# Weights turned during the forward pass, a PSUM bank for each half of the mixing, small loads on ScalarE's queue and an earlier table load, in a Hartley and AFNO expert kernel

## The chip, the cores and the metric

The kernel runs on one core of a Trainium2 chip. The metric is the device time of one execution in microseconds (us). A core has five engines that run side by side, each with its own instruction queue: TensorE (PE, matrix products into PSUM), VectorE (DVE), ScalarE (ACT), GpSimd (POOL) and SyncE (SP, here used to issue transfers). Any of ScalarE, GpSimd and SyncE can issue a transfer (DMA) between the chip's memory and SBUF; 16 DMA engines move the data.

## The reference

The input x is 16 images of 64 channels, 128 x 128 pixels, in float32 (67 MB). The reference first applies a spectral convolution and then an AFNO block with a mixture of experts:

```python
# spectral convolution: Hartley transform, 20 x 20 modes kept, weights w1 (64 x 64 x 20 x 20)
dht_2d(x) = fftn(x, axes=(2, 3)).real - fftn(flip(x, axis=(2, 3)), axes=(2, 3)).imag
x1n, x2n = _neg_k(x1), _neg_k(x2)
e = lambda a, b: einsum('bixy,ioxy->boxy', a, b)
mixed = 0.5 * (e(x1, x2) - e(x1n, x2n) + e(x1, x2n) + e(x1n, x2))
# (blurred along all four axes)
...
# the block
h = _group_norm(x, gn1_w, gn1_b)
h = _afno(h, afno_w1, afno_b1, afno_w2, afno_b2)
h = h + residual
...
feats = _gelu(_c1(h, fe_w, fe_b))
# shared and gated experts on feats
```

`_neg_k` maps the mode k to -k, so the mixing needs the weights twice: as they are, and turned.

## The kernel before

The kernel is one program with four stages that follow each other.

**Stage 1, the forward transform** (L194 to L263). The input comes in 128 tiles `xt` of 128 x 1024 (512 KB; a ring of 10 buffers, loaded by SP at L245). For each tile TensorE forms 16 small products with `fwd1` (L250) into one of four PSUM buffers, and ScalarE copies the result into `t1` (L253). Once the eight tiles of an image are done, a generator `along_columns` does the transform along the columns, interleaved with the tiles of the next image: TensorE L210 (with the table `fwd2`, loaded at L258 once the first image's tiles have been issued), ScalarE L215, VectorE L219 to L223, and then the blur over the images, which VectorE adds into `x2` (L231, L233). When an image of `x2` is complete, ScalarE writes its second half (L236, L237). At the end of the loop SP loads eleven rows of mixing weights into the lower 64 partitions of `wk` (L261).

**Stage 2, the mixing** (L265 to L341). Eleven rows of weights for the mode -k come into `wn` (L271, four buffers) and are copied in reversed order into the upper partitions of `wk` (L273, L274), by POOL for even rows and by ScalarE for odd rows. Then SP issues the transfer of `dev` (a table of the group norm) and 34 small loads (L276 to L301): `blurc`, `mean`, `gn1`, `ident`, `sel`, `vec` and 28 pieces of the AFNO weights. For each of the eleven rows k1 TensorE forms 20 products (L314) of 64 columns into one PSUM tile `psm`: the lower half of the partitions for even modes, the upper half for odd modes, both in one bank. ScalarE copies the lower half out (L318, L321, L322) and VectorE the upper half (L319, L323) to `om`. The channel blur (L332) turns `om` into `ot`, with copies on both engines (L339, L341). After it the table `spec` (3.2 MB, 100 partitions) and the expert weights `exw` are loaded (L344, L345).

**Stage 3, group norm statistics and AFNO** (L348 to L621). TensorE forms means (L420), deviations with `dev` (L430; ScalarE squares them, L432) and their sum (L436). A chain on VectorE gives the scales `gx` (L457 to L487). Then a loop over the 16 images: products of `ot` and `spec` (L599) in two halves of 512 columns, VectorE's scaled copy `xk` (L603) and ScalarE's plain copy `xr` (L604), both read from PSUM, then two AFNO layers (L537 to L552) and steps that prepare the inverse transform.

**Stage 4** (from L624) is the inverse transform, the features, the gate and the experts, in an order written out by hand: rows (L678), pixels (L704), features (L764), experts (L858 on TensorE, L863 on ScalarE, L866 on VectorE) and the stores (L877).

Each engine runs its instructions in the order of the program; a buffer that is used again waits for its last reader. Memory of a pool that is closed can be given to a later pool, whose first writer then waits for the last reader of the old one.

Of the kernel before, what the change touches and what calls it, by code (L numbers as in the profile page):

```python
# [11 lines left out]
F32 = mybir.dt.float32  # L12
AF = mybir.ActivationFunctionType
ALU = mybir.AluOpType
AX = mybir.AxisListType
PSUM = bass.MemoryType.PSUM
DRAM = bass.MemoryType.DRAM

NB, C, N = 16, 64, 128
K = 20  # L20
NM = K * K
CH = 100
MD = 32
W1 = 64
NE, TOPK = 16, 4
# [5 lines left out]
CL = C // 2  # L31
# [5 lines left out]
V_B1, V_SHB, V_EXB = 15, 17, 19  # L37
V_N = V_EXB + NE
# [120 lines left out]
def hartley_afno_moe_kernel(ctx: ExitStack, tc: tile.TileContext, a: dict, out: bass.AP):  # L159
    nc = tc.nc  # L160
# [11 lines left out]
        return t  # L172

    on_modes = ExitStack()
    otp = on_modes.enter_context(tc.tile_pool(name="ot", bufs=1, side="right"))
    ot = otp.tile([CH, 4, NB * C], F32, name="ot")

    od = dram.tile([NB, K, C, K], F32, name="od")
    ond = dram.tile([NB, K, C, K], F32, name="ond")
# [4 lines left out]
    exd = dram.tile([NE, C, C + 1], F32, name="exd")  # L184


    with tc.tile_pool(name="modes", bufs=1) as mp:


# [2 lines left out]
        wk = mp.tile([P, K // 2 + 1, K, C], F32, name="wk")  # L192
        gb = blur_matrix(NB)
        with tc.tile_pool(name="f_x", bufs=10) as xp, tc.tile_pool(name="f_t", bufs=2) as tp, \  # L194
                tc.tile_pool(name="f_c", bufs=1) as fc, \
                tc.tile_pool(name="f_p1", bufs=4, space=PSUM) as pp1, \
                tc.tile_pool(name="f_p2", bufs=2, space=PSUM) as pp2:
            fwd1 = load(fc, "fwd1", [P, W1], nc.gpsimd)
# [62 lines left out]
                nc.sync.dma_start(wk[0:C, k], a["w"][k])  # L261
            for _ in behind:
                pass  # L263

        with tc.tile_pool(name="m_o", bufs=1) as op, tc.tile_pool(name="m_w", bufs=4) as wp, \  # L265
                tc.tile_pool(name="m_p", bufs=2, space=PSUM) as pp, \
                tc.tile_pool(name="m_p2", bufs=4, space=PSUM) as pp2:

            for k in range(K // 2 + 1):
                wn = wp.tile([P, K, C], F32, name="wn")  # L270
                nc.sync.dma_start(wn[C:P], a["w"][(-k) % K])  # L271
                copy = nc.scalar.copy if k % 2 else nc.gpsimd.tensor_copy
                copy(wk[C:P, k, 0], wn[C:P, 0])  # L273
                copy(wk[C:P, k, 1:K], wn[C:P, K - 1:0:-1])  # L274
            sc = on_modes.enter_context(tc.tile_pool(name="s_c", bufs=1, side="right"))
            blurc = load(sc, "blurc", [P, C])  # L276
            dev = load(sc, "dev", [CH, 4, NM])
            mean = load(sc, "mean", [CH, 4, C])
            gn1 = load(sc, "gn1", [P, 2, C])
            ident = load(sc, "ident", [P, C])  # L280
            sel = load(sc, "sel", [CH, 5, 32])
            vec = load(const, "vec", [P, V_N])
            wx1 = sc.tile([P, 2, CL], F32, name="wx1")
            wx2 = sc.tile([P, 2, 2, CL], F32, name="wx2")
            bx1 = sc.tile([P, 2], F32, name="bx1")
            bx2 = sc.tile([P, 1], F32, name="bx2")
            v2s = a["v2"].rearrange("p (r h c) -> p h r c", r=2, h=2)
            for h in range(2):
                hs_ = slice(h * CL, (h + 1) * CL)
                for ri in range(2):  # L290
                    own_rows = slice(h * C + ri * CL, h * C + (ri + 1) * CL)
                    for ro in range(2):
                        c0 = (ri ^ ro) * P + h * CL
                        nc.sync.dma_start(wx1[own_rows, ro], a["w1"][hs_, c0:c0 + CL])
                    nc.sync.dma_start(bx2[own_rows], a["b2"][0:1, ri * C + h * CL:ri * C + (h + 1) * CL]
                                      .rearrange("a c -> c a"))
                    for j in range(2):
                        rows_j = slice(j * C + ri * CL, j * C + (ri + 1) * CL)
                        nc.sync.dma_start(wx2[rows_j, h],
                                          v2s[ri * C + h * CL:ri * C + (h + 1) * CL, h])  # L300
                        nc.sync.dma_start(bx1[rows_j, h:h + 1], a["vec"][hs_, V_B1 + ri:V_B1 + ri + 1])  # L301

            om = [op.tile([P, NB, NM // 2], F32, name=f"om{h}") for h in range(2)]
            lok, upk = (t[h * C:(h + 1) * C].rearrange("o b (k2 k1) -> o k1 k2 b", k1=K)
                        for h, t in enumerate(om))
            for k1 in range(K // 2 + 1):

                ps = pp.tile([P, K // 2, 2, NB, 2], F32, name="psm")  # L310
                for m in range(K // 2):
                    k = k1 * K + 2 * m
                    for h in range(2):
                        nc.tensor.matmul(ps[h * C:(h + 1) * C, m].rearrange("p a b q -> p (a b q)"),  # L314
                                         lhsT=wk[:, k1, 2 * m + h, :], rhs=x2[:, :, :, k:k + 2],
                                         start=True, stop=True)
                lo, up = ps[0:C, :, :, :, 0], ps[C:P, :, :, :, 1]
                nc.scalar.copy(lok[:, k1], lo[:, :, 0])  # L318
                nc.vector.tensor_copy(upk[:, k1], up[:, :, 0])  # L319
                if k1 % (K // 2):  # L320
                    nc.scalar.copy(lok[:, K - k1, 0:1], lo[:, 0:1, 1])  # L321
                    nc.scalar.copy(lok[:, K - k1, K // 2 - 1:0:-1], lo[:, 1:, 1])  # L322
                    nc.vector.tensor_copy(upk[:, K - k1, ::-1], up[:, :, 1])  # L323


            for b0 in range(0, NB, 8):
                for cc in range(2):
# [7 lines left out]
                    for h in range(2):  # L335
# [3 lines left out]
                            nc.scalar.copy(dst, src)  # L339
                        else:  # L340
                            nc.vector.tensor_copy(dst, src)  # L341

    sc2 = on_modes.enter_context(tc.tile_pool(name="s_c2", bufs=1, side="right"))
    spec = load(sc2, "spec", [CH, 4, 2 * MD * MD])  # L344
    exw = load(sc2, "exw", [P, C, NE])  # L345


    s3 = ctx.enter_context(ExitStack())  # L348
    pool = lambda name, bufs, **kw: s3.enter_context(tc.tile_pool(name=name, bufs=bufs, **kw))
# [44 lines left out]
    with tc.tile_pool(name="s_o", bufs=1) as so, \  # L394
# [3 lines left out]
        ones = sc.tile([P, C], F32, name="ones")  # L398
        nc.vector.memset(ones, 1.0)

        ext = sc.tile([C, NE, C + 1], F32, name="ext")
        nc.gpsimd.tensor_copy(ext[:, :, 0:C], exw[0:C].rearrange("p o e -> p e o"))
        nc.gpsimd.tensor_copy(ext[:, :, C], vec[0:C, V_EXB:V_EXB + NE])
        nc.gpsimd.dma_start(exd.rearrange("e i o -> i e o"), ext)
# [179 lines left out]
            return bn1s, bn1f, bn2s, bn2f  # L584

        sw = sq_pool.enter_context(tc.tile_pool(name="s_w", bufs=2))
        junk = sc.tile([P, MD * MD], F32, name="junk")
        first = second = None
        for b in range(NB):
            xk = sw.tile([P, MD * MD], F32, name="xk")  # L590
            xr = sw.tile([P, MD * MD], F32, name="xr")
            for n in range(2):
                cols = slice(n * 512, (n + 1) * 512)
                ps = pp2.tile([P, 512], F32, name="psx")
                for kc in range(4):
                    for h in range(2):
                        for ri in range(2):
                            p0 = h * C + ri * CL
                            nc.tensor.matmul(  # L599
                                ps[p0:p0 + CL], lhsT=ot[:, kc, b * C + h * CL:b * C + (h + 1) * CL],  # L600
                                rhs=spec[:, kc, ri * 1024 + n * 512:ri * 1024 + (n + 1) * 512],
                                start=(kc == 0), stop=(kc == 3))
                nc.vector.tensor_scalar(xk[:, cols], ps, gx[:, 0, b:b + 1], None, ALU.mult)  # L603
                nc.scalar.copy(xr[:, cols], ps)  # L604
                if n == 0:
                    nc.vector.tensor_scalar(xk[:, 0:1], xk[:, 0:1], gx[:, 1, b:b + 1], None, ALU.add)
                    if first:
                        second = layer1(*first)
                elif second:
                    layer2(*second)  # L610
            first = (b, xk, xr)
            if b == HB:
                bn1s, bn1f, bn2s, bn2f = prepare()
            if b < K // 2:
                modes(b)
            elif b < K // 2 + QB:
                modes_out(b - K // 2)
# [377 lines left out]
```

## Time and profile before

| | |
|---|---|
| three runs, median | 1709.37 us (1701.23 to 1716.32) |
| profiled execution, its own time | 1706.11 us |
| its span in the profile | 1704.3 us |
| mean granted TensorE clock | 0.972 |
| TensorE busy | 1564.1 us (92%) |
| ScalarE busy | 1314.3 us (77%) |
| VectorE busy | 1234.9 us (72%) |
| GpSimd busy | 153.3 us (9%) |
| first copy of stage 1 (L253) starts | 8.00 us |
| mixing's products (L314) run on from | 249.00 us |
| spectrum's products (L599) start | 311.80 us |
| stage 4 (L678) starts | 473.93 us |

The page also cuts the span in 40 equal slices of 42.6 us and gives the busy share of each in tenths (9 is 90% or more). The first six or seven slices are stages 1 and 2, the next four stage 3:

```profile
PE   6878758899978999999999999999999999999986
DVE  0344423455433888898988889898888889889998
ACT  2233334356656999999999999999999999999986
DMA  9899964333532425162442616244151533513123
```

The page's groups of instructions are read as: line, engine, operation, what it writes <- what it reads, shape, count | busy time in us, mean duration in ns | the idle time just before them, and what ended most of it. "issue" is time in which an engine waited for nothing that the profile shows. A line such as "SPq L245 <- PE ps L250" says that the transfer queue of SP, at line 245, waited for TensorE's instruction of line 250.

### The profile page before, as it was taken

How to read it: one execution, taken by the hardware profiler on the slowest of the kernel's cores; microseconds unless marked ns; L12 is line 12 of the kernel's file. 1: busy time of each engine (PE TensorE's matmuls, PEld its weight loads, DVE VectorE, ACT ScalarE, POOL GpSimd, SP SyncE). 2: the span in 40 equal slices, each digit the busy share in tenths (PEclk: the TensorE clock that was granted, in tenths of full speed). 3: DMA queues.
4: the chain of work that ended last, by engine and by line, in shares of the span. 5: the costliest groups of instructions: out<-in, count | busy, mean ns of one | idle time of the engine just before them, and what ended most of it. 6: DMA issues, size and time to landing. Idle time of an engine off the chain costs nothing.

```text
span 1704.3 us, 69104 instructions
## 1 busy us (share of the span) xinstructions
PE 1564.1 (92%) x31336; PEld 841.1 (49%) x31336; DVE 1234.9 (72%) x1584; ACT 1314.3 (77%) x1679; POOL 153.3 (9%) x137
## 2 busy tenths in 40 slices
PE   6878758899978999999999999999999999999986
PEld 6877755222276454545445454544545444454321
DVE  0344423455433888898988889898888889889998
ACT  2233334356656999999999999999999999999986
POOL 0000002002100110101011010101101011010110
PEclk9999979999988999999999999999999999999988
DMA  9899964333532425162442616244151533513123
GB/s 386 306 313 313 304 140 105 87 97 105 150 75 38 76 67 112 31 136 48 94 84 60 111 30 136 51 90 92 53 111 52 114 70 74 112 31 100 40 69 99
DMA packets 268973, 194.36 MB, mean 114 GB/s; under 512 B 228128, under 2 KB 229232, under 8 KB 268452
## 3 DMA queue, kind: packets, MB, share of 16 engines
q1 hardware_dynamic: 264984, 184.23, 42.7%
q0 software_dynamic: 3696, 5.71, 1.3%
q8 instruction: 246, 4.03, 1.0%
q14 instruction: 47, 0.39, 0.1%
HBM read 106.66 MB, written 83.23 MB: 111 GB/s over the span
## 4 chain that ended last, share of the span: by engine, by line
PE 84%; issue 7%; DVE 4%; ACT 2%; DMA 1%; POOL 0%; SPq 0%; DVEq 0%; POOLq 0%; ACTq 0%
PE pe L858 36%; PE pe L704 11%; PE pe L678 9%; PE psx L599 7%; PE pe L764 7%; PE ps L250 6%; PE ps L210 3%; DVE h L866 2%; PE psx L430 1%; PE pso L537 1%; PE pso L549 1%; DMA fwd_sb<-in_fwd_dram 1%; PE psd L517 1%; ACT g L863 1%; PE psm L314 0%
## 5 line engine op out<-in xcount | busy, mean ns | idle before, releaser
L866 DVE SCALAR_TENSOR_TENSOR h<-g,wt,h 128x1024 f32<-128x1024 f32 x512 | 625.3, 1279 | 53.7 <-ACT g L863 52.9
L863 ACT ACTIVATE g<-pe,wl 128x1024 f32<-128x1024 f32 x512 | 543.6, 1156 | 14.7 <-PE pe L858 14.0
L858 PE MATMUL pe<-f,wl 64*64 64x512 f32 x4096 | 498.3, 601 | 5.2 <-DMA wl<-exd,ati 3.2
L866 DVE SCALAR_TENSOR_TENSOR h<-g,h 128x1024 f32<-128x1024 f32 x256 | 300.9, 1216 | 37.6 <-ACT g L863 26.1
L863 ACT ACTIVATE g<-pe,vec_sb 128x1024 f32<-128x1024 f32 x256 | 274.0, 1116 | 26.6 <-PE pe L858 24.8
L858 PE MATMUL pe<-f,shw 64*64 64x512 f32 x2048 | 253.0, 602 | 0.0
L858 PEld LDWEIGHTS pe<-f,wl 64*64 64x64 f32 x4096 | 134.0, 132 | 231.5 <-ACT g L863 141.1
L704 PEld LDWEIGHTS pe<-inv_sb,u 64*64 64x64 f32 (+1 forms) x8192 | 195.8, 135 | 80.4 <-ACT g L863 52.3
L704 PE MATMUL pe<-inv_sb,u 64*64 64x128 f32 (+1 forms) x8192 | 203.7, 248 | 1.2 <-ACT u L685 1.2
L250 PE MATMUL ps<-fwd_sb,xt 128*64 128x64 f32 x4096 | 156.0, 233 | 34.7 <-issue 27.9
L678 PEld LDWEIGHTS pe<-inv_sb,bmf 64*64 64x64 f32 x4096 | 131.9, 137 | 85.2 <-issue 31.3
L678 PE MATMUL pe<-inv_sb,bmf 64*64 64x64 f32 x4096 | 152.6, 226 | 18.3 <-issue 16.4
L250 PEld LDWEIGHTS ps<-fwd_sb,xt 128*64 128x64 f32 x4096 | 145.5, 148 | 38.5 <-issue 31.5
L253 ACT COPY t<-ps 128x320 f32<-128x320 f32 x128 | 53.9, 426 | 141.7 <-PE ps L250 141.5
L685 ACT COPY u<-pe 128x1024 f32<-128x1024 f32 x128 | 130.8, 1042 | 36.3 <-PE pe L678 35.3
L678 PE MATMUL pe<-inv_sb,bmh 52*64 52x64 f32 x4096 | 146.6, 223 | 7.8 <-issue 7.8
L768 ACT ACTIVATE f<-pe,fba 128x1024 f32<-128x1024 f32 x128 | 145.7, 1170 | 3.0 <-PE pe L764 2.3
L710 DVE COPY h<-pe 128x1024 f32<-128x1024 f32 x64 | 78.4, 1225 | 74.3 <-PE pe L704 69.4
L764 PE MATMUL pe<-h,fsa 64*64 64x512 f32 x1024 | 131.7, 602 | 0.0
L678 PEld LDWEIGHTS pe<-inv_sb,bmh 52*64 52x64 f32 x4096 | 125.7, 137 | 10.4 <-issue 10.2
L831 POOL TENSOR_TENSOR dv<-root_e,dv 128x4 f32<-128x4 f32 x16 | 31.8, 1989 | 1038.1 <-DVE dv L830 1038.1
L599 PE MATMUL psx<-spec_sb,ot 100*32 100x512 f32 x1024 | 117.7, 602 | 7.4 <-issue 7.4
(181 smaller groups left out, 1112.5 us busy)
## 6 DMA issues: line engine op xcount, KB each, us to landing
xt<-in_x_dram SPq DMA_DIRECT2D x128, 512.0 KB
out_dram<-h SPq DMA_DIRECT2D x256, 256.0 KB
td<-tt SPq DMA_DIRECT2D x16, 512.0 KB
bmf<-td SPq DMA_DIRECT2D x16, 512.0 KB
bmh<-od SPq DMA_DIRECT2D x96, 50.0 KB
tnd<-tn SPq DMA_DIRECT2D x32, 128.0 KB
bmf<-td SPq DMA_DIRECT2D x32, 128.0 KB
bmf<-tnd SPq DMA_DIRECT2D x32, 128.0 KB
```

Source lines behind the costliest of these rows:

```text
L250: nc.tensor.matmul(ps[cols, i, :], lhsT=xt[:, i, cols], rhs=fwd1, start=True, stop=True)
L253: nc.scalar.copy(t1[:, :, c0:c0 + 8], src)
L599: nc.tensor.matmul(ps[p0:p0 + CL], lhsT=ot[:, kc, b * C + h * CL:b * C + (h + 1) * CL], rhs=spec[:, kc, ri * 1024 + n * 512:ri * 1024 + (n ...
L678: nc.tensor.matmul(ps[s * C:(s + 1) * C, h, i, part, :], lhsT=bmh[rs, c] if part else bmf[rs, c].rearrange("p r m -> p (r m)"), rhs=inv1[r ...
L685: nc.scalar.copy(dst, ps.rearrange("p h i q n -> p n q h i"))
L704: nc.tensor.matmul(to, lhsT=u[rs, (t * 4 + j) * 2 + half, part], rhs=by, start=(part == 0), stop=(part == 1))
L710: (nc.vector.tensor_copy if t % 2 else nc.scalar.copy)(h, ps)
L764: nc.tensor.matmul(ps[p * C:(p + 1) * C, half], lhsT=fsa[rows_, box["b"]], rhs=box["h"][t][rows_, p], start=True, stop=True)
L768: nc.scalar.activation(f, ps, AF.Gelu, bias=fba[:, box["b"]:box["b"] + 1], accum_out=box["sums"][:, t:t + 1])
L858: nc.tensor.matmul(ps[half * C:(half + 1) * C, p], lhsT=w[rows_], rhs=f[rows_, half], start=True, stop=True)
L863: nc.scalar.activation(g, ps, AF.Gelu, bias=bias)
L866: nc.vector.scalar_tensor_tensor(h, g, share(), h, ALU.mult, ALU.add)
```

## The change

The change has six parts.

1. A new pool `s_k` is opened ahead of everything, and the 34 small loads are issued by ScalarE at the very start of the program, instead of by SP in stage 2. Space for `ot` is taken only after the forward pass.
2. The loads of `wn` and the turning copies stand in the forward pass, after its last loads, with three buffers of a pool opened beside the x tiles (before: four buffers, in stage 2).
3. The mixing uses two PSUM tiles, `psm0` and `psm1`, one for each half; each product has 32 columns (its own modes only) instead of 64.
4. `dev`, `spec` and `exw` are loaded at the head of stage 2. `dev` and `spec` get memory that the pools of the forward pass held: in the built program `spec` waits for the last readers of the forward pass, and `dev` for the last turning copy; `dev` stands behind `spec` in SP's order.
5. `ext` and `junk`, two work tiles of stage 3, lie in other pools.
6. In the loop over images ScalarE's copy `xr` comes first, and VectorE's `xk` is made from `xr` in SBUF instead of from PSUM.

On ScalarE the program has 34 more instructions, on SP 34 fewer; on the other engines the numbers are unchanged. From L678 on the order on every engine is as before. The diff, cut:

```diff
     on_modes = ExitStack()
-    otp = on_modes.enter_context(tc.tile_pool(name="ot", bufs=1, side="right"))
-    ot = otp.tile([CH, 4, NB * C], F32, name="ot")
+    sk = on_modes.enter_context(tc.tile_pool(name="s_k", bufs=1, side="right"))
...
+    blurc = load(sk, "blurc", [P, C], nc.scalar)
+    mean = load(sk, "mean", [CH, 4, C], nc.scalar)
+    gn1 = load(sk, "gn1", [P, 2, C], nc.scalar)
+    ident = load(sk, "ident", [P, C], nc.scalar)
+    sel = load(sk, "sel", [CH, 5, 32], nc.scalar)
+    vec = load(const, "vec", [P, V_N], nc.scalar)
...
+                nc.scalar.dma_start(wx1[own_rows, ro], a["w1"][hs_, c0:c0 + CL])
...
-                tc.tile_pool(name="f_c", bufs=1) as fc, \
+                tc.tile_pool(name="f_c", bufs=1) as fc, tc.tile_pool(name="f_w", bufs=3) as wp, \
...
             for _ in behind:
                 pass
-
-        with tc.tile_pool(name="m_o", bufs=1) as op, tc.tile_pool(name="m_w", bufs=4) as wp, \
-                tc.tile_pool(name="m_p", bufs=2, space=PSUM) as pp, \
-                tc.tile_pool(name="m_p2", bufs=4, space=PSUM) as pp2:
-
             for k in range(K // 2 + 1):
                 wn = wp.tile([P, K, C], F32, name="wn")
                 nc.sync.dma_start(wn[C:P], a["w"][(-k) % K])
                 copy = nc.scalar.copy if k % 2 else nc.gpsimd.tensor_copy
                 copy(wk[C:P, k, 0], wn[C:P, 0])
                 copy(wk[C:P, k, 1:K], wn[C:P, K - 1:0:-1])
...
+        otp = on_modes.enter_context(tc.tile_pool(name="ot", bufs=1, side="right"))
+        ot = otp.tile([CH, 4, NB * C], F32, name="ot")
+        sc = on_modes.enter_context(tc.tile_pool(name="s_c", bufs=1, side="right"))
+        dev = load(sc, "dev", [CH, 4, NM])
+        sc2 = on_modes.enter_context(tc.tile_pool(name="s_c2", bufs=1, side="right"))
+        spec = load(sc2, "spec", [CH, 4, 2 * MD * MD])
+        exw = load(sc2, "exw", [P, C, NE])
...
-                ps = pp.tile([P, K // 2, 2, NB, 2], F32, name="psm")
+                ps = [pp.tile([P, K // 2, 2, NB], F32, name=f"psm{h}") for h in range(2)]
...
-                        nc.tensor.matmul(ps[h * C:(h + 1) * C, m].rearrange("p a b q -> p (a b q)"),
-                                         lhsT=wk[:, k1, 2 * m + h, :], rhs=x2[:, :, :, k:k + 2],
+                        nc.tensor.matmul(ps[h][h * C:(h + 1) * C, m].rearrange("p a b -> p (a b)"),
+                                         lhsT=wk[:, k1, 2 * m + h, :], rhs=x2[:, :, :, k + h],
                                          start=True, stop=True)
-                lo, up = ps[0:C, :, :, :, 0], ps[C:P, :, :, :, 1]
+                lo, up = ps[0][0:C], ps[1][C:P]
...
-        ext = sc.tile([C, NE, C + 1], F32, name="ext")
+        ext = so.tile([C, NE, C + 1], F32, name="ext")
...
-        junk = sc.tile([P, MD * MD], F32, name="junk")
+        sw1 = sq_pool.enter_context(tc.tile_pool(name="s_w1", bufs=1))
+        junk = sw1.tile([P, MD * MD], F32, name="junk")
...
-                nc.vector.tensor_scalar(xk[:, cols], ps, gx[:, 0, b:b + 1], None, ALU.mult)
                 nc.scalar.copy(xr[:, cols], ps)
+                nc.vector.tensor_scalar(xk[:, cols], xr[:, cols], gx[:, 0, b:b + 1], None, ALU.mult)
```

More of the change, by code (lines that the diff above doesn't have):

```diff
@@ L184, in hartley_afno_moe_kernel @@
     exd = dram.tile([NE, C, C + 1], F32, name="exd")
+    blurc = load(sk, "blurc", [P, C], nc.scalar)
[4 more added lines that the diff above has]
+    vec = load(const, "vec", [P, V_N], nc.scalar)
+    wx1 = sk.tile([P, 2, CL], F32, name="wx1")
+    wx2 = sk.tile([P, 2, 2, CL], F32, name="wx2")
+    bx1 = sk.tile([P, 2], F32, name="bx1")
+    bx2 = sk.tile([P, 1], F32, name="bx2")
+    v2s = a["v2"].rearrange("p (r h c) -> p h r c", r=2, h=2)
+    for h in range(2):
+        hs_ = slice(h * CL, (h + 1) * CL)
+        for ri in range(2):
+            own_rows = slice(h * C + ri * CL, h * C + (ri + 1) * CL)
+            for ro in range(2):
+                c0 = (ri ^ ro) * P + h * CL
+                nc.scalar.dma_start(wx1[own_rows, ro], a["w1"][hs_, c0:c0 + CL])
+            nc.scalar.dma_start(bx2[own_rows], a["b2"][0:1, ri * C + h * CL:ri * C + (h + 1) * CL]
+                              .rearrange("a c -> c a"))
+            for j in range(2):
+                rows_j = slice(j * C + ri * CL, j * C + (ri + 1) * CL)
+                nc.scalar.dma_start(wx2[rows_j, h],
+                                  v2s[ri * C + h * CL:ri * C + (h + 1) * CL, h])
+                nc.scalar.dma_start(bx1[rows_j, h:h + 1], a["vec"][hs_, V_B1 + ri:V_B1 + ri + 1])
     with tc.tile_pool(name="modes", bufs=1) as mp:
@@ L274, in hartley_afno_moe_kernel @@
                 copy(wk[C:P, k, 1:K], wn[C:P, K - 1:0:-1])
[L275 to L301, printed above, removed]
+        otp = on_modes.enter_context(tc.tile_pool(name="ot", bufs=1, side="right"))
@@ new lines, in hartley_afno_moe_kernel @@
+        ot = otp.tile([CH, 4, NB * C], F32, name="ot")
[4 more added lines that the diff above has]
+        exw = load(sc2, "exw", [P, C, NE])
+        with tc.tile_pool(name="m_o", bufs=1) as op, \
+                tc.tile_pool(name="m_p", bufs=2, space=PSUM) as pp, \
+                tc.tile_pool(name="m_p2", bufs=4, space=PSUM) as pp2:
@@ L341, in hartley_afno_moe_kernel @@
                             nc.vector.tensor_copy(dst, src)
-    sc2 = on_modes.enter_context(tc.tile_pool(name="s_c2", bufs=1, side="right"))
-    spec = load(sc2, "spec", [CH, 4, 2 * MD * MD])
-    exw = load(sc2, "exw", [P, C, NE])
     s3 = ctx.enter_context(ExitStack())
```

## The prediction

> **What bounds the kernel now.** I read the chain of waits first, then the 40 slices, then the waits of the load queue SP, then the start of each engine's timeline. Stage 4 holds most of the span (L678 begins at 473.93 us), and the change leaves its order of work alone. So I follow only 0 to 474 us. From the chain, the pieces around the change (start, length, what):
>
> ```profile
> 243.10 4.05 DMA wn<-in_w_dram
> 249.00 4.54 PE psm L314 x79
> 273.45 4.00 PE pst L332 x201
> 283.40 17.41 PE psx L430 x40
> 300.82 3.63 PE psd L436 x16
> 304.45 7.35 issue
> 311.80 8.76 PE psx L599 x64
> ```
>
> The mixing waits for the first turned weight, and the spectrum stands 7.35 us for its table: SP sees that table land only then (its row below). The waits of SP (total, times, longest) and two rows of the costliest groups:
>
> ```profile
> SPq L245 <- PE ps L250: 138.6, 109, 4.4
> SPq L366 <- DMA spec_sb<-in_spec_dram: 20.9, 1, 20.9
> SPq L271 <- DVE x L231: 23.0, 1, 23.0
> SPq L245 <- DMA xt<-in_x_dram: 10.9, 14, 1.1
> ...
> L250 PE MATMUL ps<-fwd_sb,xt 128*64 128x64 f32 x4096 | 156.0, 233 | 34.7 <-issue 27.9
> L253 ACT COPY t<-ps 128x320 f32<-128x320 f32 x128 | 53.9, 426 | 141.7 <-PE ps L250 141.5
> ```
>
> In the forward pass SP waits 138.6 us for TensorE to give tiles back and only 10.9 us for their data; ScalarE waits 141.5 us for TensorE. So TensorE paces it, and TensorE's own stops are "issue". A delay of TensorE here is not won back from the loads. Windows (stretch, then PE, PEld, DVE, ACT, POOL busy, clock, DMA share, GB/s):
>
> ```profile
> 10.00:20.00 10.00, 8.23 (x247) 8.04 (x246) 0.00 (x0) 2.69 (x7) 0.00 (x0) 1.00 1.03 415
> 20.00:40.00 20.00, 14.48 (x416) 13.98 (x412) 3.06 (x11) 4.91 (x12) 0.00 (x0) 0.91 1.02 406
> 40.00:180.00 140.00, 111.74 (x3426) 109.02 (x3428) 55.39 (x144) 44.82 (x105) 0.00 (x0) 0.95 0.91 313
> ```
>
> **What the Trainium skill says.** "Runtime: NRT & Kernel Launch", Instruction fetch mechanics: instructions arrive in 16 KiB blocks of 256 by a DMA ring of their own, mostly hidden. The trace has 246 such packets of 4.03 MB (16.4 KB each), and "issue" stops at 28.51, 34.88, 199.7, 221.41 us and so on: here not hidden. "DMA: Bandwidth & Descriptors", How many engines (k): a transfer spreads over the largest divisor of its slowest dimension up to 16. A table of 100 rows then uses 10 engines. The trace agrees: spec's 3.2 MB took 24.5 us, 131 GB/s, beside 406 GB/s of x tiles. Same page, Issuing engines are not separate DMA queues: issuing from another engine saves sequencer time only. So the small loads moved to ScalarE gain no bandwidth; they move about 17 us of issuing. "PSUM — Partial Sum Buffer", Specifications: ScalarE and VectorE read it together at full rate unless they meet in a bank. Before, both halves lie in one bank, and the trace has L321 waiting for DVE's L319 9 times for 0.5 us.
>
> **The change part by part.** T is the end of the forward pass (the last x2 half, L237, ends at 246.52). All sums are against the profiled execution, 1706.11 us; the median shown is 1709.37, from 1701.23 to 1716.32, so this execution sits 3.3 below it.
>
> *1. 34 small loads at the head of ScalarE's queue.* On SP their issues took, from the rows of the same loads: six first ones 0.58+0.30+0.36+0.43+0.36+0.33 = 2.4; L294 8×0.42 = 3.4; L295 4×0.42 = 1.6; L299 8×0.57 = 4.6; L301 8×0.58 = 4.6. Together 16.6 us. In the built program a load also waits for an earlier one on a shared set of eight semaphores: ScalarE's 23rd for the sixth x tile, its 26th and 30th for the next two, its last for fwd2. Queued behind it on ScalarE: the activation table load (1.28 us) and then every copy of L253. The first copy ran here:
>
> ```profile
> 8.00 0.42 ACT L253 COPY t<-ps 128x320 f32<-128x320 f32 x1 [5.99 <-PE ps L250]
> ...
> 18.18 1.52 PE L210 MATMUL ps<-fwd_sb,t 128*64 128x64 f32 x45 [0.77 <-DMA fwd_sb<-in_fwd_dram]
> ```
>
> Lowest: 0.7 start + 16.6 + 1.28 = 18.6, and the fwd2 landing (18.18 before) + wait and table load gives 20.3; I take that as the lower end. The x tiles now go two at a time instead of eight, so fwd2 lands later: I take 21.5, and the first copy at **23**; upper end 27 (eight loads in flight at the 5.7 us that the slowest wn load took: 34/8 × 5.7 = 24.2, + 2 + 0.7). TensorE has four PSUM buffers at L250, fills them by 9.7 us and stops until 23.4: 13.7 lost. Of this it wins back what it lost before in that stretch: 0.77 for fwd2, 1.00 and 1.15 of issue stops at 16.14 and 22.25, and 1.5 because from 20 to 40 us it ran 72% busy under full DMA against 80% later, and the tiles now lie ready (20 × 0.07). That is 4.4, so **+9.3** (bounds +4: copy at 20.3 and more fetch stops hidden; +14: copy at 27). The 16.6 us leave SP behind the wn loads, where they pushed spec to 287.18.
>
> *2. Weights turned during the forward pass.* wn0 to wn2 wait only for the wk loads (issued 209.1 to 220.1), so they transfer by about 236, beside TensorE's last instruction blocks (the 4.08 us stop at 221.41 shows what crowding does). Price: +1 (0 to +3). Their turning copies are 1.4 us each; POOL is idle, and ScalarE's stand behind the last x2 halves, at T. wn3 waits for POOL's copy of row 0, wn4 for ScalarE's copy of row 1, both by T+1; so from row 4 loads follow at 4 to 5.7 us latency, as before.
>
> *3. Mixing.* It starts at T+0.1 instead of T+2.5 (249.00) and has rows 0 to 3 ready. Bank per half: the collisions of L321 (4.5 us) and waits DVE L323 <- ACT L322 (5.0) shrink, but these alternate; matmuls on 32 columns cost at most half of L314's 1.38 us per 20 pairs less. The last copy, before at T+27.4, then stands at wn10: wn4 at T+1.5, wn7 about T+8, wn10 about T+14.5, landed T+19, turned T+20.5, mixed T+22. **-5.4** (-2 to -6.5) for this stage by itself.
>
> *4. dev and spec.* SP issues spec behind wn10, T+14.5; 24.5 us long, so it lands at T+38.5 to 39, before at 311.7 = T+65.2. But dev now lies in memory that the wn buffers held: it waits for the last turning copy (about T+20.5) and stands behind spec in SP's queue. Before, it was issued at 262.51 and waited for nothing. Its 0.64 MB over the same ten engines queue behind spec: landing about **T+42** (T+25 if its packets pass spec's; T+46 if exw goes between). L430's matmuls need it. By the mixing alone they could start at T+22+9.4 (the 9.4 being last copy to L430 before, 273.9 to 283.33), T+31.4; they stand 10.6 us and start at T+42, before T+36.8.
>
> *5. The spectrum.* L430 and L436 take 21.1 us (283.33 to 304.45), so it starts at T+63.1 with no wait for spec, before T+65.3. The scale gx needs 10.5 us from 304.48, 1.7 of them a wait for fold, which now lands earlier. With the swap of L603 and L604, ScalarE empties PSUM without gx, so TensorE need not stop; without the swap it could lose 8.8 - 2×4.4 = 0. Beyond, a batch is 10.04 us, dense on TensorE: DVE's read from SBUF instead of PSUM (747 ns before) lies beside it, 0 (-2 to +1). ext and junk moved: 0, POOL waited 32.5 us for exw there and nothing near follows.
>
> Steps 3 to 5 come to T+63.1 against T+65.3: **-2.2** (-13 if dev lands in time; +3 if it lands at T+46 or after). Sum: +9.3 +1 -2.2 = **+8.1**, 1714.2 in the profiled execution, 1717.5 from the median. I state **1716**, between the two.
>
> **Rivals.**
> (a) *The gains land* (chance 0.14): dev passes spec and TensorE wins back most of the start. For: packets of both share engines; TensorE had 41.8 us of issue stops in L250 and L210 to shrink. Against: one queue, issue order. +4 +0 -13 = -9: 1697 to 1700. Faster by over 1% needs a start that costs nothing, -17 in all.
> (b) *Slower* (0.17): ScalarE's queue is held through landings, each small load in line behind half-megabyte tiles. With eight in flight at 7 us each (two tiles and what stands between) 34/8 × 7 = 29.8, + 2 + 0.7: copy at 32, forward +18; with -2.2 and +1 it is +17, 1726. It decides from a first copy at 31 us. For: the shared set of semaphores, and full DMA engines until 40 us. Against: small loads took 1.6 to 3.5 us beside the weights, and most of these go before any wait for a tile.
> (c) *The bank and column part does nothing* because wn10 ends the mixing anyway (inside the central case; +2 if wn's chain is no shorter than before, 1718).
>
> **Numbers.** Central case 0.69, (a) 0.14, (b) 0.17. One per cent, 17 us, is about what a measurement of this kernel can tell from no change: faster is below 1692, slower above 1726.5. Central bounds: +4+0-6 and +14+3+1 give 1707 to 1727; with (a) and half of (b) outside, the range is 1700 to 1730. Faster 0.06, same 0.75, slower 0.19.
>
> **What would show it.** Step 1: the first L253 copy at 20 to 27 us, a hole in TensorE from 9.7, x2's last half 8 to 13 us after 246.5. Step 2: wn landings before T. Step 3: last om copy at T+20 to T+24. Step 4: idle time ahead of the L430 matmuls, released by dev, of 5 to 14 us; spec landed at T+36 to T+42. Step 5: no idle time ahead of the spectrum. From there to the end the two traces should be equal within 3 us. It is wrong if TensorE catches up by 180 us, or if dev lands before the mixing ends.

## The result and the profile after

The changed kernel takes 1723.2 us (median of 11 runs, 1720.98 to 1727.69), the kernel before 1706.06 us (11 runs, 1701.01 to 1716.32). The ratio is 1.0100, with a 95% interval of 1.0079 to 1.0122: it is slower, by about the one per cent that the prediction took as the bound of what counts. The profiled execution of the changed kernel took 1726.48 us with a span of 1724.7, 20.4 above the span of before.

The loss lies ahead of stage 4. Its rows start at 493.94 us instead of 473.93, 20.0 later; from there to the end both traces need the same time, 1230.8 and 1230.4 us. The chain of waits of the changed kernel from the end of the forward pass (start, length, what; short pieces left out; its first line is the last `x2` half):

```profile
263.19 0.53 ACT x L262
...
263.82 4.25 PE psm L316 x80
...
270.21 5.25 DMA wn<-in_w_dram
...
276.92 4.64 DMA wn<-in_w_dram
...
282.98 1.57 PE psm L316 x25
...
284.56 25.67 DMA dev_sb<-in_dev_dram
...
310.27 19.98 PE psx L427 x40
330.26 3.58 PE psd L433 x16
333.84 7.00 PE psx L597 x64
```

The forward pass ends at 263.72 instead of 246.52, so 17.2 us are lost in it. In the chain of before there stood a stop of 7.35 us for `spec`; it is gone, and in its place stands a transfer of `dev` that takes 25.67 us. The chain enters that transfer at 284.56, the moment when the last buffer of the turned weights came free (POOL's last turning copy ends at 284.53, beside the product that the chain names). It is long because it lies behind `spec`: the profile's packets show the first piece of `dev` moving at 300.5, 16 us after its issue, while those of `spec` move from 280.8 to 304.2. In e9 below, where `dev` is issued ahead of `spec`, its first piece moves 0.9 us after its issue.

The start of the forward pass, ScalarE's timeline (start, length, engine or its transfer queue, line, operation; in brackets the idle time before it and what ended it):

```profile
26.07 0.57 ACTq L208 DMA_DIRECT2D wx<-in_v_dram  x1
26.68 0.59 ACTq L210 DMA_DIRECT2D bx<-in_vec_dram  x1
27.30 1.28 ACT L278 ACT_TABLE_LOAD   x1 [27.30 <-DMA bx<-in_vec_dram]
28.60 1.41 ACT L278 COPY t<-ps 128x320 f32<-128x320 f32 x4
```

and TensorE's:

```profile
7.55 5.75 PE L275 MATMUL ps<-fwd_sb,xt 128*64 128x64 f32 x128 [7.55 <-DMA fwd_sb<-in_fwd_dram]
29.08 7.14 PE L275 MATMUL ps<-fwd_sb,xt 128*64 128x64 f32 x192 [15.78 <-ACT t L278]
```

TensorE fills four PSUM buffers and stands 15.78 us for ScalarE, whose first copy runs at 28.60 instead of 8.00. The four copies that had piled up then take 1.41 us.

TensorE's timeline from the channel blur to the spectrum:

```profile
287.78 5.19 PE L334 MATMUL pst<-blurc_sb,om 64*64 64x64 f32 x213 [0.33 <-ACT om L320]
298.56 1.50 PE L334 MATMUL pst<-blurc_sb,om 64*64 64x64 f32 x43 [5.59 <-issue]
299.99 6.17 PE L417 MATMUL psd<-ot,mean_sb 100*64 100x512 f32 x16
310.27 19.98 PE L427 MATMUL psx<-ot,dev_sb 100*100 100x512 f32 x40 [4.11 <-DMA dev_sb<-in_dev_dram]
330.19 3.65 PE L433 MATMUL psd<-sq,ones 100*64 100x512 f32 x16
```

The same products in the kernel before:

```profile
278.96 0.81 PE L332 MATMUL pst<-blurc_sb,om 64*36 64x64 f32 x41 [1.51 <-issue]
279.70 3.71 PE L420 MATMUL psd<-ot,mean_sb 100*64 100x512 f32 x16
283.33 17.48 PE L430 MATMUL psx<-ot,dev_sb 100*100 100x512 f32 x40
300.75 3.65 PE L436 MATMUL psd<-sq,ones 100*64 100x512 f32 x16
```

Ahead of the deviations three things are longer: the stop inside the blur (5.59 against 1.51 us, no releaser but "issue"), the blur's products on both sides of it (5.19 and 1.50 against 4.00 and 0.81) and the means (6.17 against 3.71). Only 4.11 us are a wait for `dev`. The deviations themselves take 19.98 instead of 17.48 us.

Put together, with T for the end of the forward pass (last half of `x2`); the "last om copy" ends the mixing:

| | before | after | difference |
|---|---|---|---|
| T | 246.5 | 263.7 | +17.2 |
| T to last om copy | 27.4 | 24.2 | -3.1 |
| last om copy to deviations | 9.4 | 22.3 | +12.9 |
| deviations to spectrum, the wait for spec with it | 28.5 | 23.5 | -5.0 |
| spectrum's loop to stage 4 | 162.1 | 160.2 | -2.0 |
| stage 4 | 1230.4 | 1230.8 | +0.4 |

The -2.0 in the loop is no gain of the swapped copies as such. The spectrum's first 64 products take 8.76 us before, where they follow a wait, and 7.07 after, where they follow other products. e12 below has the swap and a wait of 2.94 us there: its first 64 products take 8.77 us and its loop 162.2.

### The profile page after: what moved, and what is told of

Same layout as the page of the kernel before. It is cut to its first block, busy times and chain, and to the rows that moved or that the text cites. A ratio compares the mean times of both kernels' runs of the same rounds, so it can differ in the third digit from the quotient of the medians.

```text
span 1724.7 us, 69109 instructions
## 1 busy us (share of the span) xinstructions
PE 1564.3 (91%) x31336; PEld 840.7 (49%) x31336; DVE 1228.1 (71%) x1584; ACT 1314.2 (76%) x1679; POOL 155.1 (9%) x137
## 4 chain that ended last, share of the span: by engine, by line
PE 74%; issue 4%; DVE 2%; DMA 2%; ACT 2%; POOL 0%; DVEq 0%; ACTq 0%
PE pe L856 36%; PE pe L702 11%; PE pe L676 8%; PE psx L597 7%; PE pe L762 7%; DVE h L864 2%; DMA dev_sb<-in_dev_dram 1%; PE psx L427 1%; PE pso L546 1%; PE pso L534 1%; ACT g L861 1%; DMA wn<-in_w_dram 1%; PE psd L514 1%; PE psm L316 0%; PE pa L779 0%
## 5 line engine op out<-in xcount | busy, mean ns | idle before, releaser
L864 DVE SCALAR_TENSOR_TENSOR h<-g,h 128x1024 f32<-128x1024 f32 x256 | 301.1, 1216 | 37.7 <-ACT g L861 27.9
L244 DVE TENSOR_TENSOR xm<-ps,pn 64x20 f32<-64x20 f32 x32 | 5.5, 171 | 173.2 <-ACT pn L240 173.0
```

The source lines that it names most:

```text
L864: nc.vector.scalar_tensor_tensor(h, g, share(), h, ALU.mult, ALU.add)
```

## The experiments

The kernel before takes 1678 us in some rounds of runs and 1706 to 1710 in others. Why is not known: the record gives the same chip number, 2, for rounds of both kinds. The difference lies in stage 4 (1230.4 us in the trace of before, 1203.7 in that of the first run below, with the same order of work). So whole times are compared as ratios to the kernel before in the same round, and the traces by the times ahead of stage 4.

To see where the forward pass loses, the start of the n-th copy of an x tile out of PSUM (there are 128) is compared with the kernel before. Lag in us, read from ScalarE's timelines:

| copy (before at) | after | small loads alone (e2) | ScalarE later (e5) | weights spread (e8) | loads back on SP (e9) |
|---|---|---|---|---|---|
| 1 (8.0) | +20.6 | +19.4 | +2.8 | +0.1 | 0.0 |
| 9 (20.8) | +14.6 | +14.0 | +9.5 | +0.4 | +0.1 |
| 57 (105.5) | +14.0 | +14.2 | +11.7 | +23.0 | -1.5 |
| 113 (200.4) | +15.1 | +14.6 | +14.2 | +34.5 | -1.5 |
| 125 (226.6) | +19.4 | +14.8 | +16.0 | +28.4 | +0.2 |
| 128 (234.7) | +17.9 | +14.5 | +16.1 | +25.8 | +1.2 |

The first two columns say it at a glance: the delay is there by the ninth copy, the next 100 copies win none of it back, and the changed kernel loses 2.8 us more after copy 113, where the small loads alone lose nothing.

**e1: the small loads on SP, spread over the x tiles.**

```diff
-    blurc = load(sk, "blurc", [P, C], nc.scalar)
...
+                    if b >= 1:
+                        next(rest, None)      # one small load, nc.sync
```

> The changed kernel with the 34 small loads taken from the head of ScalarE's queue and issued by SP, one beside each x tile from the second image on. Theory A (ScalarE's queue at the start costs the loss of the forward pass): first copy of L253's kind at 7.5 to 9 us instead of 28.60, the last x2 half ends at 247 to 250 instead of 263.7, and the rest of the program follows at the same distance: 1706 to 1710 us, 14 to 17 below the changed kernel. Theory B (small loads in front of or among the x tiles starve the forward pass, whichever queue issues them, since all loads share eight semaphores): the forward pass still ends after 256, 1715 or more.

Ratio 1.0044 (1.0031 to 1.0057). The first copy runs at 7.98 us, the forward pass ends at 250.7, and stage 4 starts at 481.35, 12.6 before that of the changed kernel. So theory A holds for most of the forward pass, and B is out: the same loads beside the x tiles leave the lag near zero up to the 89th copy. But 4 us of the forward pass stay lost, A's total is missed (14 to 17 us below the changed kernel would be a ratio of 1.000 to 1.002), and the spectrum stands 70.5 us after T, as in the changed kernel (70.1). The wait for `dev` is there again (5.56 us), and so is the stop in the blur (5.29).

**e2: the small loads at the head of ScalarE's queue, in the kernel before.** The blocks of part 1 of the change alone; `dev` keeps its place on SP.

> The kernel before with one part of the change alone: the 34 small loads at the head of ScalarE's queue. Theory A: first copy at 27 to 30 us, forward pass 14 to 17 us longer (x2 ends at 260 to 264); spec is issued right after the mixing instead of 12 us later and its 7.35 us wait goes; total +7 to +10 against before. Theory C (the loss of the forward pass comes from the weight loads and turning copies inside it): forward pass 3 us longer at most, and with spec earlier the kernel is 4 us faster than before.

Ratio 1.0060 (1.0038 to 1.0082), stage 4 9.7 us later than before. From ScalarE's timeline, the first copy and the last `x2` half:

```profile
27.37 1.41 ACT L280 COPY t<-ps 128x320 f32<-128x320 f32 x4
...
259.81 0.52 ACT L264 COPY x<-x 64x400 f32<-64x400 f32 x1
```

T is 260.3, 13.8 later: one part of the change makes most of its loss of 17.2 us in the forward pass, and about half of its loss of 20.0 at stage 4. C's 3 us bound fails. `spec` is issued 36.5 us after T instead of 40.7 and the wait ahead of the spectrum falls from 7.4 to 3.25, less than the 7.35 that was expected to go.

**e3: all turning copies on POOL.**

```diff
-                copy = nc.scalar.copy if k % 2 else nc.gpsimd.tensor_copy
+                copy = nc.gpsimd.tensor_copy
```

> The changed kernel with all turning copies on POOL, none behind ScalarE's last copies of the forward pass. Theory A (transfers of dev and spec wait for wn's buffers, whose turning copies stand in ScalarE's queue until the forward pass ends): forward pass unchanged (ends at 262 to 265), wn10 issued before or within 3 us of its end, spec lands at about 27 to 32 us after it instead of 42, dev about then instead of 46.5, the deviations start 33 to 36 us after it, the spectrum at 55 to 58 instead of 70: 1709 to 1713. Theory D (TensorE's products and instruction fetch set the stretch from the mixing to the spectrum, dev's wait only covers them): 1720 to 1724.

Ratio 1.0029 (1.0015 to 1.0044). The forward pass ends at 267.2, somewhat later than expected. From there the expectation of A holds: wn10, the last of the eleven rows of turned weights, is issued at 266.04, the last om copy stands 16.9 us after T instead of 24.2, `dev` lands 30.8 us after T instead of 46.5, and the spectrum starts 55.6 after it. TensorE's timeline:

```profile
293.52 1.54 PE L334 MATMUL pst<-blurc_sb,om 64*36 64x64 f32 x45 [5.36 <-issue]
294.99 6.92 PE L417 MATMUL psd<-ot,mean_sb 100*64 100x512 f32 x16
301.84 17.48 PE L427 MATMUL psx<-ot,dev_sb 100*100 100x512 f32 x40
```

No wait for `dev` is left ahead of L427, but the stop of 5.36 us inside the blur stays. That is D's part of the story: both theories hold a share.

**e4: dev in memory of its own.**

```diff
+            dev = load(sk, "dev", [CH, 4, NM])
             for k in range(K // 2 + 1):
                 wn = wp.tile([P, K, C], F32, name="wn")
...
-        dev = load(sc, "dev", [CH, 4, NM])
```

> The changed kernel with dev in memory of its own, loaded ahead of the wn rows, so that it waits for no turning copy. Theory A: the deviations no longer wait 4.1 us for dev; with the 5.6 us stop of TensorE inside the channel blur still there, the spectrum starts 4 to 9 us sooner: 1714 to 1720. If that stop is instruction fetch behind dev's and spec's packets it stays, since spec is still issued in the same place. Theory D: 1722 to 1725.

Ratio 1.0079 (1.0057 to 1.0100); stage 4 starts 5.4 us sooner than in the changed kernel, inside A's 4 to 9. The wait for `dev` is gone and the spectrum stands 61.7 us after T; T itself is 266.7, 3 later; the transfer of `dev` now lies in the end of the forward pass (its packets move from 243.5 to 251.9), but e3, e6 and e7 end it as late without that, so the 3 us are not shown to be its price. The stop in the blur stays at 4.67 us.

**e5: the small loads on ScalarE, but later.** The same statements as in e1, with ScalarE as the issuing engine.

> The changed kernel with the 34 small loads still issued by ScalarE, but ten of them ahead of its first copy of the forward pass and the others one or two behind each of the following copies. Theory A (only what stands ahead of the first copies costs): first copy at 8 to 12 us, forward pass ends at 250 to 254 as with SP (250.7), ratio to before 1.003 to 1.006. Theory E (issuing on ScalarE itself holds the copies up and with them TensorE, wherever it stands): forward pass ends after 257, ratio 1.008 or more.

Ratio 1.0077 (1.0049 to 1.0106): A's number is missed, and T = 263.0 is what E said. The first copy runs at 10.80, as expected, but the lag is 5.3 at the eighth copy and 9.5 at the ninth. ScalarE's timeline shows the last step; ten loads stand in one block ahead of the ninth copy, which is not the even spacing that the expectation assumed:

```profile
22.78 0.42 ACT L283 COPY t<-ps 128x320 f32<-128x320 f32 x1 [2.09 <-PE ps L280]
...
29.39 0.32 ACTq L207 DMA_DIRECT2D bx<-in_vec_dram  x1
29.76 0.47 ACT L446 ACTIVATE wx<-wx 32x32 f32<-32x32 f32 x2 [6.55 <-DMA wx<-in_v_dram]
30.25 0.42 ACT L283 COPY t<-ps 128x320 f32<-128x320 f32 x1
```

So a gap of 7 us between two copies adds 4.2 us of lag: it is not only what stands ahead of the first copy that costs. E (issuing on ScalarE costs wherever it stands) is not ruled out, since no run spread the loads evenly. The lag grows by another 4.7 us up to copy 113; where that comes from was not settled.

**e6: one bank and 64 columns, on top of e3.**

```diff
-                ps = [pp.tile([P, K // 2, 2, NB], F32, name=f"psm{h}") for h in range(2)]
+                ps = pp.tile([P, K // 2, 2, NB, 2], F32, name="psm")
```

and the products and copies of the kernel before.

> The run with all turning copies on POOL, and the mixing back to one PSUM tile for both halves and products of 64 columns. Theory F (with the weights ready, the bank and the columns set the pace of the mixing): rows take 2 to 2.2 us instead of 1.2, the last copy stands 23 to 26 us after the forward pass instead of 17, the spectrum 60 to 64 instead of 55.6, ratio 1.006 to 1.009 instead of 1.0029. Theory G (the stop for instructions inside the channel blur ends with spec's transfer and takes the difference up): the spectrum at 55 to 58, ratio 1.002 to 1.005.

Ratio 1.0048 (1.0030 to 1.0065) against 1.0029 for e3; the two intervals overlap, and G's range of ratios holds, not F's. In the traces the mixing needs 22.0 us instead of 16.9, and the spectrum starts 58.2 us after T instead of 55.6. The waits of e6 inside the mixing (line waiting, for whom, total, times, longest):

```profile
ACT om L323 <- DVE om L321: 4.7, 9, 0.5
DVE om L325 <- ACT om L324: 4.4, 8, 0.6
PE psm L316 <- DVE om L325: 3.8, 4, 1.1
```

In e3 none of these three stands in the waits. The products themselves take 237 ns with 64 columns and 244 with 32. So a tile and bank per half is worth 5 us where the weights are ready, and the columns nothing. The waits are for the other engine's copy out of the same tile; whether a second tile in the same bank would have been enough was not tried. Half of the 5 us arrives: e3 gives back 1.8 in the means (6.92 us at a granted clock of 0.53, against 5.09 at 0.71).

**e7: xk first, as before.**

```diff
-                nc.scalar.copy(xr[:, cols], ps)
-                nc.vector.tensor_scalar(xk[:, cols], xr[:, cols], gx[:, 0, b:b + 1], None, ALU.mult)
+                nc.vector.tensor_scalar(xk[:, cols], ps, gx[:, 0, b:b + 1], None, ALU.mult)
+                nc.scalar.copy(xr[:, cols], ps)
```

> The changed kernel with the order of the two copies in the spectrum's loop as before (VectorE's xk from PSUM first, then xr). Theory H (the swap lets TensorE run on while gx is not there, and is where stage 3 won 2 us): from the first products of the spectrum to the first rows of stage 4 it takes 162 us again instead of 160.2, and more if TensorE must wait for gx, ratio 1.010 to 1.013. Rival: the swap does nothing, 160.2 stays.

Ratio 1.0128 (1.0086 to 1.0171). From the spectrum to stage 4 it takes 165.1 us instead of 160.2. TensorE's timeline shows the stop:

```profile
346.05 5.34 PE L597 MATMUL psx<-spec_sb,ot 100*32 100x512 f32 x32 [2.41 <-ACT xr L602]
```

ScalarE's `xr` waits behind VectorE's `xk`, which waits for `gx`; TensorE stands 2.4 us, and the next 32 products take 5.34 instead of 3.62. H's numbers hold: in the order of the changed kernel, where the spectrum no longer waits for its table, the swap is worth 4.9 us in the trace.

**e8: the weights and dev through the forward pass**, on top of e1 and e3.

```diff
+                if b == 2:
+                    dev = load(sk, "dev", [CH, 4, NM])
+                if 2 <= b < K // 2 + 3:
+                    k = b - 2
+                    nc.sync.dma_start(wk[0:C, k], a["w"][k])
+                    wn = wp.tile([P, K, C], F32, name="wn")
+                    nc.sync.dma_start(wn[C:P], a["w"][(-k) % K])
...
```

> The changed kernel with the small loads on SP beside the x tiles, all turning copies on POOL, and dev and both sets of weights loaded through the forward pass, one row of each per image from the third on. Theory A: nothing but x tiles at the end of the forward pass, which ends at 245 to 250; the mixing follows at 1.2 us a row, spec is issued at the end of the forward pass and lands 25 to 28 us after it, the spectrum starts 52 to 56 us after it, at 298 to 305: ratio 0.991 to 0.996. Rival C (the weights' bytes and POOL's copies cost the forward pass wherever they stand in it): it ends after 253, ratio 0.997 or more.

Ratio 1.0109 (1.0079 to 1.0139): A is wrong, C right. T is 271.8. The stage after it is the shortest of all (the spectrum 48.7 us after T), but the lag grows to 7.1 us at the 25th copy and 34.5 at the 113th. TensorE's waits over the whole run:

```profile
PE ps L280 <- issue: 47.4, 19, 5.2
```

Before, that row had 27.9. With the column transform's products, whose stops got shorter, TensorE's "issue" stops in the forward pass are 56.2 us against 41.8, so 14.4 of the 25.3 us lost. The weights' transfers and turning copies cost the forward pass also where they are spread over it. (The profiled execution, 1685.79 us, lies 10 below this kernel's median.)

**e9: small loads on SP behind the wn rows, turning on POOL.** The changed kernel with e3's edit and with the small loads moved:

```diff
-    blurc = load(sk, "blurc", [P, C], nc.scalar)
...
+        blurc = load(sk, "blurc", [P, C], nc.sync)     # behind the wn loads, ahead of dev
```

> The changed kernel with the 34 small loads on SP behind the wn loads and all turning copies on POOL; dev and spec follow the small loads on SP. Theory A: first copy at 8 us, forward pass ends 3 to 6 us later than before (249 to 253, the price of the wn loads inside it), spec is issued some 17 us after it and lands at 41 to 46 us after it, behind the channel blur, so that the stop for instructions inside the blur shrinks from 5.4 to 2 us or less; the spectrum starts 50 to 56 us after the forward pass, at 300 to 308: ratio 0.992 to 0.998. Rival (spec is late again and its wait comes back): the spectrum at 310 or later, ratio 0.999 or more.

Ratio 0.9931 (0.9907 to 0.9955): it beats both kernels. T = 248.9, the last om copy 16.1 us later, the stop in the blur 1.80 us. `spec` is issued at 273.78, behind the blur, the spectrum starts at 303.73 and stage 4 at 463.90, 10.0 ahead of the kernel before. TensorE's timeline and, below it, the chain of waits, with what is left, a wait for `dev`:

```profile
270.72 0.92 PE L333 MATMUL pst<-blurc_sb,om 64*36 64x64 f32 x46 [1.80 <-issue]
...
280.59 19.62 PE L426 MATMUL psx<-ot,dev_sb 100*100 100x512 f32 x40 [5.34 <-DMA dev_sb<-in_dev_dram]
```

```profile
273.38 7.17 DMA dev_sb<-in_dev_dram
280.59 19.62 PE psx L426 x40
300.22 3.58 PE psd L432 x16
```

**e10: the kernel before with the bank, the swap and the turning on POOL** (the edits of e3, and the reverse of e6 and e7).

> The kernel before with two parts of the change, a bank per half with 32 columns and ScalarE's copy xr first, and all turning copies on POOL; loads as before. Theory A (these parts were worth something, the others took it back): forward pass ends at 246 to 248, the last om copy 20 to 24 us after it instead of 27, spec is issued at 275 to 281 instead of 287 and the spectrum starts at 299 to 306; from there 160 us to stage 4 instead of 162: ratio 0.990 to 0.995. Rival (spec's landing does not move, since the small loads in front of it on SP set it): the spectrum at 309 or later, ratio 0.997 or more.

Ratio 0.9976 (0.9962 to 0.9989): the rival's prediction, a gain of a quarter of a per cent. The small loads on SP end at 286.8 and `spec` is issued at 287.01; the spectrum starts at 310.94. The mixing, too, did not get shorter: the last copy stands 26.6 us after T. The windows of this kernel (stretch, PE, PEld, DVE, ACT, POOL busy, clock, DMA share, GB/s) show it:

```profile
260.00:265.00 5.00, 5.00 (x98) 5.00 (x98) 2.25 (x6) 2.04 (x9) 4.73 (x9) 0.50 0.87 209
265.00:270.00 5.00, 5.00 (x98) 5.00 (x98) 1.54 (x5) 1.49 (x6) 2.34 (x3) 0.50 0.66 178
```

TensorE has no gap left, its granted clock is 0.50 and a row takes 2.1 us. In the kernel before, with its gaps, the clock is 1.00 from 255 us on.

**e11: the same without the turning on POOL.**

> The kernel before with a bank per half and 32 columns and with ScalarE's copy xr first, nothing else. Theory A: the turning copies on ScalarE still set the pace of the mixing, which ends 24 to 27 us after the forward pass; spec lands 0 to 3 us sooner, the loop takes 160 us instead of 162: ratio 0.996 to 0.999. Rival (the bank sets the pace by itself): the mixing ends at 22 us or less, ratio 0.995 or less.

Ratio 1.0001 (0.9984 to 1.0019). The mixing ends 27.0 us after T, `spec` is issued at 288.37, and the clock is 0.50 from 245 to 280 us as in e10. A's small gain does not show: alone, these two parts bring nothing to the kernel before that the runs can tell.

**e12: e9 with dev in memory of its own**, issued between the wn rows and the small loads.

```diff
+        dev = load(sk, "dev", [CH, 4, NM])
         blurc = load(sk, "blurc", [P, C], nc.sync)
...
-        dev = load(sc, "dev", [CH, 4, NM])
```

> The run with the small loads on SP and the turning on POOL, and dev in memory of its own, so that it is issued right behind the last wn row instead of behind the small loads. Theory A: dev lands before the mixing ends and the 5.3 us wait ahead of the deviations goes; they start at 272 to 277 and take 17.5 us instead of 19.6; spec, issued at about 274 without dev in front of it, lands at 298 to 300 and sets the start of the spectrum at 298 to 301 instead of 303.7: ratio 0.988 to 0.992, 3 to 6 us below the run without it. Rival (dev's packets beside the last wn rows delay the turning and the blur): the spectrum at 303 or later, ratio 0.993 or more.

Ratio 0.9912 (0.9887 to 0.9938), on another chip than e9's (12, not 2); the intervals overlap, so it is not shown to be better than e9. The wait for `dev` is gone, and `spec`'s landing sets the spectrum, in TensorE's timeline:

```profile
280.32 17.48 PE L426 MATMUL psx<-ot,dev_sb 100*100 100x512 f32 x40
297.73 3.65 PE L432 MATMUL psd<-sq,ones 100*64 100x512 f32 x16
304.33 8.77 PE L596 MATMUL psx<-spec_sb,ot 100*32 100x512 f32 x64 [2.94 <-DMA spec_sb<-in_spec_dram]
```

The spectrum stands 50.2 us after T against 54.8 in e9, but this execution's forward pass ended 5 us later (254.1), so the expected start at 298 to 301 is missed. The lag is there from the 89th copy on, where the two kernels have the same work. So a single trace's T is known to some 5 us only: e9, e12, and the kernels with the unchanged small loads in front (263.7 to 269.0 in after, e3, e4, e6 and e7) all show that spread.

## Why the prediction was right and where its steps failed

The stated range of 1700 to 1730 held the median, and the kernel is slower by one per cent, the edge of "within 1%". The stated 1716 was 7 too low. In the profiled execution the sum said +8.1 and it was +20.0 at stage 4, more than the +18 of its own upper bounds (14, 3 and 1): the forward pass lost 6.9 more than the +10.3 of steps 1 and 2, the stretch from T to the spectrum took 7.0 more (70.1 instead of 63.1), and the loop behind it 2.0 less. That the range held the median owes something to its width.

1. **The start.** The mechanism was right: ScalarE's first copy late, TensorE full after four groups, nothing won back after the first copies. The size failed in one term, the 16.6 us of issuing. It added the durations of the 34 rows, and took the waits between them as small. But the trace of before already showed the whole sequence on SP, from 261.88 us to the issue of `spec` at 287.18, 25.3 us. Put into the same sum, 0.7 + 25.3 + 1.28 gives a copy at 27.3; it was 28.60. On ScalarE 19.5 us were issuing and 7.1 lay between issues, so a part of rival (b) came true, though not up to its 31 us; in its numbers, +18 for the forward pass and 1726, (b) was nearer than the central case. A reading was off the other way: TensorE's four buffers were full at 13.30, not 9.7 (in the trace of before the fourth copy runs only at 12.44), so TensorE stood 15.78 us against 13.7. The lag was 20.6 at the first copy and 14.6 at the ninth; the winning back that was put at 4.4 was 6.0. e2 shows the part alone: +13.8.
2. **Weights in the forward pass.** Put at +1 (0 to 3). From copy 113 to copy 128 the lag grows by 2.8 us in the changed kernel and by 1.8 to 5.0 in the eight other kernels that load the wn rows there (e1, e3 to e7, e9, e12), and by -0.1 to 1.2 in the three that don't (e2, e10, e11). So the price is real, and the central 1 was too small. e8's 25 us show the same direction. That these transfers delay TensorE's instructions, as the prediction says, fits the longer "issue" stops of e8 but was not shown by itself.
3. **The mixing.** The chain of wn rows was right to the microsecond: wn10 issued 14.4 us after T (put at 14.5) and landed 19.4 (19). "Mixed T+22" failed, it was 24.2: the clock was 0.50 at the end and a row took 2.1 us. Rival (c) is not settled: e6 shows 5 us for the bank where the weights are ready, and e11 shows none in the kernel before, but there TensorE without a gap at a clock of 0.50 sets the pace, not the turned weights. In the changed kernel itself the bank was not taken back alone.
4. **dev and spec.** `dev`'s issue at T+20.8 (put at 20.5) was close. `spec` landed at T+41.9 (38.5 to 39) and `dev` at T+46.5 (42, with 46 as the upper end), 3 and 4.5 us late. But the wait for `dev` was 4.11 us, not 10.6, because TensorE was ready at T+42.4, not T+31.4: the mixing ended 2.2 us later, and the term "9.4 from last copy to L430" was 18.2. The stop in the blur grew from 1.51 to 5.59, and the products around it and the means ran longer. Behind the wait the deviations took 2.5 us more, which the 21.1 for L430 and L436 did not have.

   What the stop waits for can be read from the packets. The profile lists instruction blocks as packets of 16 KB on a queue of their own, 246 in each trace; 62672 of the changed kernel's 69109 instructions are TensorE's products and weight loads. In all twelve traces that have a stop there, the 47th of these packets belongs to it: TensorE runs on 2.3 to 3.1 us after that packet starts. In the changed kernel and in e1 and e3 to e7, with `spec` in flight during the blur and a stop of 4.7 to 5.7 us, the packet starts 1.6 to 2.8 us after TensorE has stopped (at 295.46, the stop beginning at 292.97, in the changed kernel). In before, e2, e9 and e12, where `spec` is not yet issued, and in e8, where its last packets end at 291.7, the packet starts 0.5 to 1.2 us before the stop (276.64 and 277.45 in before), and the stop is 1.5 to 2.1 us. So the stop is a wait for instructions, and in seven kernels their packet comes late. The Trainium skill, "Runtime: NRT & Kernel Launch", Instruction fetch mechanics, calls the cost of crossing into a new block mostly hidden; in this blur it was not, with stops of 1.5 to 5.7 us. That `spec`'s packets are what makes the packet late is the reading that fits; no run changed the fetch by itself.
5. **The spectrum.** Its wait went, as said. It starts 70.1 us after T instead of 63.1. The swap was costed at 0 on the ground that without it TensorE would lose nothing either; e7 shows 4.9 us without it. The loop's 2.0 us, which the sum did not have, come from the wait that is gone.

Rival (a), the gains landing, needed a start without cost. e1 takes only that cost away and is still 0.4% slower than the kernel before; e9, with the turning on POOL and `spec` behind the blur as well, is 0.7% faster.

## What to carry to other kernels

Moving transfers to an idle-looking queue moves the whole elapsed time of their sequence, waits included, ahead of whatever that engine must do next; read that time from the old queue's first to last issue, not from the sum of its rows. On an engine that empties PSUM, such a block does not belong ahead of the first copy, nor between two urgent ones; e9 put it on another queue, behind the last urgent transfers. And before a large table is loaded sooner, look at what TensorE still has to fetch while it is in flight, and whether a buffer that it reuses makes a second load wait.

## What the runs showed of the hardware

The Trainium skill, "TensorE: Matmul & The Clock Gate", Part 1: The HAM clock gate, says that TensorE runs at half its clock after idling. This agrees: in the changed kernel the granted clock was 0.50 just after the stop in the blur (298.5 to 300 us) and 0.59 over the means, which took 6.17 us against 3.71 at a clock of 1.00 before. Deviations that start after a wait for `dev` took 19.2 to 20.3 us (after, e1, e5, e7, e9), all others 17.48.

The same section says that full clock comes after about 3.4 us of sustained work; in e10 it did not:

```profile
251.22 23.68 PE L314 MATMUL psm<-x,wk 128*64 128x32 f32 x438 [0.72 <-POOL wk L274]
```

Through these 23.68 us without a gap the granted clock stayed at 0.50, and a product took 294 ns on average, against 240 in the kernel before, which has gaps and a clock of 1.00 from 255 us on; e11 shows the same with 295 ns. In e9, whose TensorE is as busy from 250 to 260 us, the clock was 0.50 for the first 2.5 us and 1.00 from 255 us on. The measurement decides for this stage; what kept the clock low in e10 and e11 was not tried.
